# A two-layer graph network on one core: some gathers row by row from SyncE, and the turn of finished sums moved inside a unit

## The chip, the core and the metric

The kernel runs on one core of a Trainium2 chip. The metric is the device time of one execution in microseconds. Three timed runs of the kernel before gave 4084.81, 4095.0 and 4096.76 us; their median is 4095.0. The core's engines are TensorE (PE, with its weight loads as PEld), VectorE (DVE), ScalarE (ACT), GpSimd (POOL) and SyncE (SP). SyncE computes nothing here: its queue issues most of the direct transfers. ScalarE issues the stores, GpSimd the gathers.

## The reference

Two message-passing layers, each followed by a residual addition and a layer norm over the 160 features of each of N = 6250 nodes. There are E = 200000 edges, ordered by target node. A layer does this (layer 1 with 10 inputs per edge and 192 weights, layer 2 with 64 inputs and 224 weights):

```python
w   = silu(edge_inputs @ W1) @ W2              # per edge, 192 or 224 weights
g   = (x @ lin1 * node_scale)[src]             # a row of 160 per edge, gathered
mid = products of pieces of w, g and the 4 edge attributes
agg = segment_sum(mid, dst, num_segments=N) / 4
out = self_part(x) + agg @ lin2                # layer 2: then silu and a sigmoid gate
x   = layernorm(x + out)
```

Targets are drawn as 6250 u^2 of a uniform u, so low nodes have many edges, and finished nodes come faster and faster towards the end of the edge list.

## The kernel before

**Tiles and units.** The edges stand in 1563 tiles of 128; four tiles are a unit (391 units), two tiles a pair, eight tiles a chunk of edge inputs (`EC`), 48 tiles a chunk of sources and attributes (`CH`). The nodes stand in 49 blocks of 128 (the last has 106). `windows(i, ...)` (L587 to L856) runs layer i. Its loop over u (L824) is a software pipeline written out by hand; each step does, in this order:

- `gather(p)` (L697) for the two pairs of unit u+4: one indirect transfer per tile on GpSimd fetches 128 rows of 160 floats from the table in DRAM into a `g` tile (eight buffers, a pair each). The indices come from `src`, which `scalars(c)` (L602) loads with the attributes `ea` when a tile first asks for its chunk.
- `weights` (L679) for unit u+2: the second matmul of the edge network into `pw` (three PSUM buffers).
- `hidden(u+3)` (L646): the first matmul into the two `pair` buffers, and ScalarE's silu. `inputs(c)` (L625) loads the chunk after the one in use into one of three `e` buffers, through SyncE.
- for both pairs of unit u+2, `places` (L726: VectorE makes `sel`, a tile that puts each edge's attributes where its target is, in a window of 32 nodes) and `products` (L708: VectorE multiplies `g` and `pw` into `mid`, four instructions in layer 1 and six in layer 2).
- for the four tiles of unit u, `aggregate(t)` (L744): four matmuls that sum `mid` by target into `pg`. Tiles form groups of 3 to 12 that share a window; at a group's last tile ScalarE copies `pg` to `r` (L759, and to `rest` in layer 2, L765).
- `turn(g)` (L768) for the groups that ended in the unit before: two transposes on TensorE into the right half of a `pair` buffer, then a window's start loaded into a VectorE register (L778) and two additions by VectorE into the running sums `sm` and `sr` (L781, L783).
- `proceed` (L816): one step of the next block of nodes whose edges are all summed. In layer 1 the steps are `summed` (L501: seven matmuls from `sm` and `sr` into `pn`, then the residual and the norm), `turn` (L520: transposes) and `mix` (L523: the linear map of layer 2, its store to the second table by ScalarE's queue, and the store of x). In layer 2 the one step `summed` (L558) ends with the store of the output.

`prepare` (L796), called in the middle of a unit's tiles, works ahead for coming blocks: `fetch` of x, `self_part` (transposes) and `self_mix`; in layer 1 it also computes the self part of the later 25 blocks (`own_nodes`, L464) and stores it to `xown`. At most two blocks stand prepared. All of these go through one PSUM buffer, `pn`.

**What sets the order.** TensorE's instructions keep the program's order (L135 to L146); the other engines' order is the scheduler's, close to the program's. After the last unit there is one more step of the loop (`units + 1`), then the remaining turns, and then the remaining blocks, one after the other (L851 to L856). Layer 2 can gather only when the last block's rows are in the second table. Direct transfers from SyncE and ScalarE share eight counters in rotation, and each waits for the one eight places before it.

Of the kernel before, what the change touches and what calls it, by code (L numbers as in the profile page):

```python
# [28 lines left out]
BG = 4  # L29
ZERO = 8  # L30
ROWS = P * NB + P
EPS = 1e-5
# [54 lines left out]
def kernel(ctx: ExitStack, tc: tile.TileContext, a, out):  # L87
# [376 lines left out]
    def own_nodes(b, work):  # L464

        n = rows_of(b)
        rows = slice(b * P, b * P + n)
        (fetch, self_part, self_mix), _ = second_nodes(b, work, False, "ne")

        def store():  # L470
            nc.scalar.dma_start(xown[rows, :], self_mix()[:n])
            owned.add(b)

        return [fetch, self_part, store]

    def second_nodes(b, work, clear, name="nx"):
# [4 lines left out]
        st = {}  # L481

        def fetch():
            x = st["x"] = work.tile([P, D], F32, name=name, bufs=4 if name == "nx" else 1)
            if b in owned:
                nc.sync.dma_start(x[:n], xown[rows, :])
            else:
                nc.sync.dma_start(x[:n], a["x_main"][:, b, :] if b < NB - 1 else a["x_tail"])
# [12 lines left out]
        def summed():  # L501
            p = psum.tile([P, 512], F32, name="pn", bufs=1)
            q = p[:n, :2 * D].rearrange("p (w d) -> p w d", w=2)
            for c in range(4):
                l = sm[:96, c, rows]
                if c < 2:
                    matmul(q[:, :, 0:S + V], l, rm0[:, c], start=(c == 0), stop=False)
                else:
                    v = S + (c - 1) * V
                    matmul(q[:, :, 0:S], l, rm0[:, c, :, 0:S], start=False, stop=False)  # L510
                    matmul(q[:, :, v:v + V], l, rm0[:, c, :, S:], start=False, stop=False)
            matmul(q[:, :, S + V:D], sr[:64, rows], rr0, start=False, stop=True)
            y = st["x"][:n]
            for k in range(2):
                nc.vector.scalar_tensor_tensor(y, q[:, k, :], gets[:n, b, k:k + 1], y,
                                               op0=OP.mult, op1=OP.add)
            mv = work.tile([P, 8], F32, name="mv")
            normed(y, mv)

        def turn():  # L520
            st["xt"] = turned(st["x"][:n], work, "pn", 1)

        def mix():  # L523
            xt = st["xt"]
            p = psum.tile([P, 512], F32, name="pn", bufs=1)
            matmul(p[:n, 0:P], xt[:, 0, :n], who[0][:, :P], start=True, stop=True)
# [11 lines left out]
    def last_nodes(b, work, clear):  # L538
# [19 lines left out]
        def summed():  # L558
# [12 lines left out]

            gate = work.tile([P, V], F32, name="gate")
            nc.scalar.activation(gate[:n], o[:, S:96], AF.Tanh, scale=half[:n, b])
            nc.vector.tensor_scalar(gate[:n], gate[:n], 1.0, half[:n, b], op0=OP.add, op1=OP.mult)
            nc.vector.tensor_tensor(
# [3 lines left out]
            nc.vector.tensor_tensor(x, y[:n], x, OP.add)  # L579
            mv = work.tile([P, 8], F32, name="mv")  # L580
            normed(x, mv)
# [4 lines left out]

    def windows(i, loads, work, inputs_of):  # L587
        nw = (192, 224)[i]
# [36 lines left out]
        def inputs(c):  # L625
# [3 lines left out]
            k, of_e = ((10, a["e10"]), (64, a["e64"]))[i]  # L629
            e = inputs_of[c % 3]  # L630

# [47 lines left out]
        def weights(ps):  # L679
# [5 lines left out]
            for p, j in [(p, j) for p in ps for j in range(2)] if i == 0 else \  # L685
                    [(p, j) for j in range(2) for p in ps]:
                t = 2 * p + j
                if t < NT:
# [6 lines left out]
                    matmul(made["w", p][:n, j, :nw], l, r, start=True, stop=True)  # L695

        def gather(p):  # L697
            g = work.tile([P, 2, D], F32, name="g", bufs=8)
            for j in range(2):
# [96 lines left out]
        def prepare():  # L796

            if early:
                early.pop(0)()
            elif not coming and left and len(prepared) < 2:  # L800
                b = left.pop(0)
# [21 lines left out]

        for u in range(-4, units + 1):  # L824
            before = turned_to
# [31 lines left out]

# [112 lines left out]
    with tc.If(ok > 0) as cmp:  # L970
        with tc.tile_pool(name="loads", bufs=2) as loads, \
                tc.tile_pool(name="edges", bufs=2) as work:

            inputs_of = [loads.tile([P, EC * P // 2], F32, name=f"e{k}", bufs=1) for k in range(3)]
            for e in inputs_of:
                nc.vector.memset(e, 0.0)
            for i in range(2):
                windows(i, loads, work, inputs_of)
    with cmp.Else():
# [56 lines left out]
```

## Time and profile before

| what | us |
|---|---|
| median of three runs | 4095.0 |
| the profiled execution's own time | 4098.1 |
| its span, first to last instruction | 4096.3 |
| first gather of layer 1 begins | 65.8 |
| last gather of layer 1 ends | 2054.8 |
| first gather of layer 2 begins | 2089.4 |
| last gather of layer 2 ends | 4057.9 |
| last store issued (out, L582) | 4091.6 |

| stretch | PE busy | DVE busy | ACT busy | POOL busy | granted clock |
|---|---|---|---|---|---|
| 500 to 600 | 88.7 | 67.8 | 22.6 | 75.9 | 0.90 |
| 1900 to 2000 | 92.8 | 76.7 | 37.5 | 76.2 | 0.95 |
| 2300 to 2400 | 81.9 | 75.8 | 13.5 | 75.9 | 0.85 |
| 3900 to 4000 | 84.9 | 88.9 | 49.1 | 75.9 | 0.96 |

The second table gives busy microseconds in stretches of 100 us. A busy TensorE is not TensorE at its peak, since the ends of its pipelined matmuls are modelled. In the views of the trace a line reads: engine, source line, operation, tile written <- tiles read, and behind it a count, a duration in nanoseconds or microseconds, or the idle time before it in brackets with what ended it. A `q` behind an engine's name means its sequencer. GpSimd's busy time is the time in which it makes the descriptors of a gather; the transfer itself runs on the DMA engines.

### The profile page before, as it was taken

Reading aid. Unit: us, or ns where it says so; the run is one execution under the profiler, and the core shown is the slowest. Engines: PE = TensorE matmul, PEld = TensorE weight load, DVE = VectorE, ACT = ScalarE, POOL = GpSimd, SP = SyncE. Lnnn points to the kernel's source line nnn. Section 1 sums busy time; section 2 is a strip of 40 time slices with the busy share of each in tenths; the row PEclk is TensorE's granted clock in tenths of the full one; section 3 lists DMA queues with packets and bytes.
Section 4 is the critical chain, followed back from the end, with each engine's and each line's share of the span. In section 5 each row is a group of like instructions: output and inputs, shape, how many; then the busy total and the mean of one; then the engine's idle time right before and its main releaser. Section 6 shows DMA issues by size and latency. Waiting matters only on the chain. (4 is left out here: it accounts for less than half of the span.)

```text
span 4096.3 us, 108196 instructions
## 1 busy us (share of the span) xinstructions
PE 3522.1 (86%) x37363; PEld 2419.1 (59%) x37363; DVE 3095.1 (76%) x13202; ACT 1176.1 (29%) x4013; POOL 3026.7 (74%) x3232
## 2 busy tenths in 40 slices
PE   7788988889899999999978888888788888888887
PEld 5565666666666666666655555555555555555555
DVE  6676666667777777777757777777778888888887
ACT  2122221222222333333311111122223333444454
POOL 4777777777777777777757777777777777777774
PEclk8899898889899999999978888889989999998998
DMA  4233322222222232333323333333333333333332
GB/s 128 78 84 87 81 75 77 78 76 79 77 79 79 79 82 79 82 84 80 87 71 94 96 95 97 98 96 96 100 97 97 103 100 96 106 100 98 101 103 59
DMA packets 298517, 364.05 MB, mean 89 GB/s; under 512 B 86323, under 2 KB 246204, under 8 KB 297964
## 3 DMA queue, kind: packets, MB, share of 16 engines
q0 software_dynamic: 151056, 257.36, 23.8%
q1 hardware_dynamic: 121740, 85.59, 7.4%
q10 hardware_dynamic: 25168, 14.11, 1.1%
q8 instruction: 300, 4.92, 0.5%
q14 instruction: 253, 2.07, 0.2%
HBM read 338.73 MB, written 18.03 MB: 87 GB/s over the span
## 5 line engine op out<-in xcount | busy, mean ns | idle before, releaser
L703 POOL DMA_INDIRECT g<-table,src x3126 | 3004.9, 961 | 1026.8 <-issue 736.9
L721 DVE TENSOR_TENSOR mid<-g,pw 128x128 f32<-128x128 f32 (+2 forms) x7820 | 1852.8, 299 | 653.0 <-DMA g<-table,src 416.1
L138 PE MATMUL pw<-fc,h 100*128 100x192 f32 (+1 forms) x6252 | 1225.5, 383 | 193.4 <-DVE mid L721 186.4
L138 PE MATMUL pg<-mid,sel 128*32 128x160 f32 (+1 forms) x25008 | 1155.1, 305 | 0.0
L138 PEld LDWEIGHTS pw<-fc,h 100*128 100x128 f32 (+1 forms) x6252 | 895.9, 203 | 369.9 <-issue 315.0
L138 PEld LDWEIGHTS pg<-mid,sel 128*32 128x32 f32 x25008 | 755.3, 116 | 387.7 <-issue 320.7
L734 DVE SCALAR_TENSOR_TENSOR sel<-iota,off,ea 128x128 f32<-128x128 f32 x3126 | 940.5, 341 | 39.4 <-PE pg L138 35.0
L138 PE MATMUL pair<-e,fc 64*100 64x256 f32 (+1 forms) x2348 | 606.2, 454 | 120.2 <-DVE sr L783 113.4
L665 ACT ACTIVATE h<-pair 100x256 f32<-100x256 f32 x782 | 260.7, 381 | 954.6 <-PE pair L138 941.0
L138 PEld LDWEIGHTS pair<-e,fc 64*100 64x100 f32 (+1 forms) x2348 | 239.5, 183 | 351.2 <-issue 193.1
L676 ACT ACTIVATE h<-pair 128x256 f32<-128x256 f32 x392 | 150.5, 384 | 960.5 <-PE pair L138 795.6
L143 PE MATMUL pair<-ident,r 128*96 128x128 f32 (+1 forms) x852 | 225.7, 291 | 27.6 <-ACT h L665 21.7
L138 PE MATMUL pn<-rm,sm 96*128 96x128 f32 (+4 forms) x980 | 192.1, 356 | 51.2 <-DVE sm L781 49.6
L759 ACT ACTIVATE r<-pg 128x96 f32<-128x96 f32 (+1 forms) x568 | 149.5, 263 | 297.8 <-PE pg L138 228.5
L781 DVE TENSOR_TENSOR sm<-pair,sm 96x128 f32 (+1 forms) x568 | 161.9, 285 | 92.1 <-PE pair L143 19.1
L143 PEld LDWEIGHTS pair<-ident,r 128*96 128x96 f32 (+1 forms) x852 | 107.8, 127 | 206.0 <-issue 105.3
L765 ACT ACTIVATE rest<-pg 32x32 f32<-32x32 f32 x1136 | 209.5, 184 | 12.5
L138 PEld LDWEIGHTS pn<-rm,sm 96*128 96x128 f32 (+3 forms) x980 | 176.3, 235 | 59.9 <-DVE sm L781 53.3
L138 PE MATMUL pn<-rr,sr 64*128 64x128 f32 (+2 forms) x196 | 66.1, 426 | 93.4 <-DVE sr L783 89.0
L458 ACT ACT_TABLE_LOAD x97 | 124.5, 1283 | 7.1 <-DVE mv L457 5.4
L138 PEld LDWEIGHTS pair<-fold,rest 128*128 128x128 f32 x568 | 104.0, 226 | 1.1 <-ACT rest L765 1.1
L783 DVE TENSOR_TENSOR sr<-pair,sr 64x32 f32 (+1 forms) x568 | 99.7, 176 | 0.8 <-DVE sm L781 0.6
(137 smaller groups left out, 1313.0 us busy)
## 6 DMA issues: line engine op xcount, KB each, us to landing
g<-table,src POOLq DMA_INDIRECT x3126
e<-in_e SPq DMA_DIRECT2D x781, 64.0 KB
e<-in_e SPq DMA_DIRECT2D x390, 20.0 KB
ea<-in_ea_main SPq DMA_DIRECT2D x63, 96.0 KB
xg<-in_x_main SPq DMA_DIRECT2D x12, 320.0 KB
table<-rg SPq DMA_DIRECT2D x12, 320.0 KB
xmid<-nx ACTq DMA_DIRECT2D x48, 80.0 KB
table<-nr ACTq DMA_DIRECT2D x48, 80.0 KB
```

The source lines that it names most:

```text
L138: r = nc.tensor.matmul(*args, **kw)
L143: r = nc.tensor.transpose(*args)
L458: nc.scalar.activation(mv[:n, 1:2], mv[:n, 1:2], AF.Sqrt, bias=eps[:n])
L665: nc.scalar.activation(h[:100, 2 * P * j:2 * P * j + m], pair[j][:100, :m], AF.Silu)
L676: nc.scalar.activation(h[:kk, c0:c1], p[:kk, c0:c1], AF.Silu, scale=0.125)
L703: nc.gpsimd.indirect_dma_start(out=g[:n, j, :], out_offset=None, in_=table[i][:, :], in_offset=bass.IndirectOffsetOnAxis(ap=of(t)[0], axis=0))
L721: nc.vector.tensor_tensor(parts(mid[:n, :m], V * place, V * step, k), parts(g[:n, :m], c, V, k), parts(q[:n, :m], w, w_step, k), OP.mult)
L734: made["last"] = nc.vector.scalar_tensor_tensor(s[:n, j], iota[:n, None, :].to_broadcast([n, 4, W]), w, e[:, :, None].to_broadcast([n, 4, ...
L759: nc.scalar.activation(r[:, :w], pg[:, :w], AF.Copy)
L765: nc.scalar.activation(rest[g % 3][k, k], pg[k, P:P + V], AF.Copy)
L781: nc.vector.tensor_tensor(sm[:h, :, at], pt[:h, :P].rearrange("p (c w) -> p c w", c=4), sm[:h, :, at], OP.add)
L783: made["last"] = nc.vector.tensor_tensor(sr[:k, at], pt[:k, P:P + W], sr[:k, at], OP.add)
```

## The change

Four things change, in one edit.

1. **Rows through SyncE.** Units 80, 160, 240 and 320 of each layer aren't gathered by GpSimd. The rows of such a unit come one by one: `rows_of_unit` spreads 64 groups over the units since the one before it; a group loads eight indices from SBUF into SyncE's registers (`row_src`, filled at the start) and issues eight transfers of one row of 640 bytes into `gs`, a tile for a unit. These keep the program's order on SyncE.
2. **Buffers and loads.** The edge inputs have two `e` buffers instead of three. Sources and attributes of the next 48 tiles are asked for when half of the chunk is gathered. `own_nodes` uses the four `no` buffers instead of one `ne`. Up to three blocks stand prepared, with the one being computed, and four for the last.
3. **The turn.** The groups that ended in the unit before are turned between the two pairs of products, in front of the unit's own sums. `proceed` stays behind the sums and is left out in the last unit; the extra step of the loop is gone.
4. **The last blocks.** The last block works in a `pw` buffer instead of `pn`, and the remaining blocks' steps are taken in turns. In the last block of layer 2 a square root on one column stands behind the gate's tanh, ahead of the norm that needs it.

```diff
+ROW_UNITS = range(80, (NT + 3) // 4 - 1, 80)
...
-        (fetch, self_part, self_mix), _ = second_nodes(b, work, False, "ne")
+        (fetch, self_part, self_mix), _ = second_nodes(b, work, False, "no")
...
+        bank = ("pn", 1) if b < NB - 1 else ("pw", 3)
+
         def fetch():
-            x = st["x"] = work.tile([P, D], F32, name=name, bufs=4 if name == "nx" else 1)
+            x = st["x"] = work.tile([P, D if name == "nx" else 192], F32, name=name, bufs=4)[:, :D]
...
         def summed():
-            p = psum.tile([P, 512], F32, name="pn", bufs=1)
+            p = psum.tile([P, 512], F32, name=bank[0], bufs=bank[1])
...
         def turn():
-            st["xt"] = turned(st["x"][:n], work, "pn", 1)
+            st["xt"] = turned(st["x"][:n], work, *bank)
...
+            if b == NB - 1:
+
+                nc.scalar.activation(mv[:n, 8:9], gates[:n, 0, 0:1], AF.Sqrt, bias=eps[:n], scale=0.0)
...
-            e = inputs_of[c % 3]
+            e = inputs_of[c % 2]
...
+        def rows_of_unit(u):
+
+            k = next((k for k, x in enumerate(ROW_UNITS) if x - 4 >= u), None)
+            begin = 0 if not k else ROW_UNITS[k - 1] - 1
+            if k is None or u < begin:
+                return
+            x = ROW_UNITS[k]
+            if u == begin:
+                made["rows", x] = work.tile([P, 4, D], F32, name="gs", bufs=1)
+            g, steps, m = made["rows", x], x - 4 - begin, P // 2
+            for q in range((u - begin) * m // steps, min((u - begin + 1) * m // steps, m)):
+                loads_, v = nc.values_load_multi_w_load_instructions(
+                    row_src[q:q + 1, k].rearrange("q h t -> q (h t)"), engines=[ET.SP], min_val=0,
+                    max_val=N - 1,
+                    skip_runtime_bounds_check_because="an edge's source is a node")
+                for r in loads_:
+                    in_order(r)
+                for h in range(2):
+                    for j in range(4):
+                        in_order(nc.sync.dma_start(g[2 * q + h:2 * q + h + 1, j, :],
+                                                   table[i][bass.ds(v[4 * h + j], 1), :]))
+
         def gather(p):
+            if p // 2 in ROW_UNITS:
+                made["g", p] = made["rows", p // 2][:, 2 * (p % 2):2 * (p % 2) + 2, :]
+                return
...
-            elif not coming and left and len(prepared) < 2:
+            elif not coming and left and len(prepared) + bool(going) < 3 + (left[0] == NB - 1):
...
-        for u in range(-4, units + 1):
+        for u in range(-4, units):
...
-            if 0 <= u + 2 < units:
-                for p in pairs_of(u + 2):
-                    places(p)
-                    products(p)
+
+            c, at = divmod(4 * (u + 4), CH)
+            if at == CH // 2 and (c + 1) * CH < NT:
+                scalars(c + 1)
+            rows_of_unit(u)
+            ps = pairs_of(u + 2) if 0 <= u + 2 < units else []
+            for p in ps[:1]:
+                places(p)
+                products(p)
+
+            ended, waiting = waiting, []
+            for g in ended:
+                turn(g)
+                turned_to = g + 1
+            for p in ps[1:]:
+                places(p)
+                products(p)
             if u >= 0:
-                ended, waiting = waiting, []
                 for t in range(4 * u, min(4 * u + 4, NT)):
...
-                for g in ended:
-                    turn(g)
-                    turned_to = g + 1
-                proceed(turned_to if u + 3 > units else before)
+                if u < units - 1:
+                    proceed(turned_to if u + 3 > units else before)
...
-        while proceed(NG):
-            pass
+
+        chains = [going] + [steps for _, steps in prepared]
+        while any(chains):
+            for steps in chains:
+                if steps:
+                    steps.pop(0)()
...
-            inputs_of = [loads.tile([P, EC * P // 2], F32, name=f"e{k}", bufs=1) for k in range(3)]
+            inputs_of = [loads.tile([P, EC * P // 2], F32, name=f"e{k}", bufs=1) for k in range(2)]
...
+            row_src = loads.tile([P // 2, len(ROW_UNITS), 2, 4], I32, name="row_src", bufs=1)
+            for k, u in enumerate(ROW_UNITS):
+                nc.sync.dma_start(row_src[:, k], a["src_main"][:, 4 * u:4 * u + 4, 0].rearrange(
+                    "(q h) t -> q h t", h=2))
```

More of the change, by code (lines that the diff above doesn't have):

```diff
@@ L516, in summed @@
                                                op0=OP.mult, op1=OP.add)
-            mv = work.tile([P, 8], F32, name="mv")
+            mv = work.tile([P, 9], F32, name="mv")
             normed(y, mv)
         def turn():
-            st["xt"] = turned(st["x"][:n], work, "pn", 1)
+            st["xt"] = turned(st["x"][:n], work, *bank)
         def mix():
             xt = st["xt"]
-            p = psum.tile([P, 512], F32, name="pn", bufs=1)
+            p = psum.tile([P, 512], F32, name=bank[0], bufs=bank[1])
             matmul(p[:n, 0:P], xt[:, 0, :n], who[0][:, :P], start=True, stop=True)
@@ L570, in summed @@
             nc.scalar.activation(y[:n, 0:S], o[:, 0:S], AF.Silu, scale=f)
-            gate = work.tile([P, V], F32, name="gate")
-            nc.scalar.activation(gate[:n], o[:, S:96], AF.Tanh, scale=half[:n, b])
-            nc.vector.tensor_scalar(gate[:n], gate[:n], 1.0, half[:n, b], op0=OP.add, op1=OP.mult)
+            gates = work.tile([P, 2, V], F32, name="gate")
+            nc.scalar.activation(gates[:n, 0], o[:, S:96], AF.Tanh, scale=half[:n, b])
+            mv = work.tile([P, 9], F32, name="mv")
+            if b == NB - 1:
+                nc.scalar.activation(mv[:n, 8:9], gates[:n, 0, 0:1], AF.Sqrt, bias=eps[:n], scale=0.0)
+            gate = gates[:, 1]
+            nc.vector.tensor_scalar(gate[:n], gates[:n, 0], 1.0, half[:n, b], op0=OP.add,
+                                    op1=OP.mult)
             nc.vector.tensor_tensor(
@@ L579, in summed @@
             nc.vector.tensor_tensor(x, y[:n], x, OP.add)
-            mv = work.tile([P, 8], F32, name="mv")
             normed(x, mv)
@@ L584, in last_nodes, with windows @@
         return [fetch, self_part, self_mix], [summed]
-    def windows(i, loads, work, inputs_of):
+    def windows(i, loads, work, inputs_of, row_src):
         nw = (192, 224)[i]
@@ L695, in weights, with in_order @@
                     matmul(made["w", p][:n, j, :nw], l, r, start=True, stop=True)
+        def in_order(r):
+            tc.keep_in_program_order(r)
+        def rows_of_unit(u):
[18 more added lines that the diff above has]
+                                                   table[i][bass.ds(v[4 * h + j], 1), :]))
         def gather(p):
+            if p // 2 in ROW_UNITS:
+                made["g", p] = made["rows", p // 2][:, 2 * (p % 2):2 * (p % 2) + 2, :]
+                return
             g = work.tile([P, 2, D], F32, name="g", bufs=8)
@@ L972 @@
                 tc.tile_pool(name="edges", bufs=2) as work:
-            inputs_of = [loads.tile([P, EC * P // 2], F32, name=f"e{k}", bufs=1) for k in range(3)]
+            inputs_of = [loads.tile([P, EC * P // 2], F32, name=f"e{k}", bufs=1) for k in range(2)]
             for e in inputs_of:
                 nc.vector.memset(e, 0.0)
+            row_src = loads.tile([P // 2, len(ROW_UNITS), 2, 4], I32, name="row_src", bufs=1)
+            for k, u in enumerate(ROW_UNITS):
+                nc.sync.dma_start(row_src[:, k], a["src_main"][:, 4 * u:4 * u + 4, 0].rearrange(
+                    "(q h) t -> q h t", h=2))
             for i in range(2):
-                windows(i, loads, work, inputs_of)
+                windows(i, loads, work, inputs_of, row_src)
     with cmp.Else():
```

## The prediction

> **What bounds the kernel now.** I read the share of busy time first, then GpSimd's costliest group, GpSimd's waits, its instructions in order of time at the edges of the two layers, and last what TensorE and VectorE wait for late in a layer.
>
> ```profile
> PE 3522.1 (86%) x37363; PEld 2419.1 (59%) x37363; DVE 3095.1 (76%) x13202; ACT 1176.1 (29%) x4013; POOL 3026.7 (74%) x3232
> ...
> L703 POOL DMA_INDIRECT g<-table,src x3126 | 3004.9, 961 | 1026.8 <-issue 736.9
> ```
>
> TensorE has the largest share, but it isn't the bound. Of GpSimd's idle time most is "issue", which is no wait. The waits (total, times, longest) and the timeline (start, length, idle before) settle it:
>
> ```profile
> POOL g L703 <- issue: 736.9, 2417, 0.3
> POOL g L703 <- DVE mid L721: 110.3, 361, 0.5
> ...
> 65.77 1.04 POOL L703 DMA_INDIRECT g<-table,src  x1 [39.56 <-DVE rr L397]
> ...
> 2053.86 0.91 POOL L703 DMA_INDIRECT g<-table,src  x1 [0.30 <-DVE nx L515]
> 2089.39 0.96 POOL L703 DMA_INDIRECT g<-table,src  x1 [34.62 <-DMA nx<-xmid]
> ...
> 4056.89 1.00 POOL L703 DMA_INDIRECT g<-table,src  x1 [0.30 <-DVE mid L721]
> ```
>
> No gap inside a layer is over 0.5 us: 0.30 us is the pitch from one gather to the next, whatever it is put down to. GpSimd issues 1563 gathers a layer end to end and waits for nobody. So the profiled execution's own 4098.1 us is a sum: 1.8 outside the span, 65.8 to the first gather, 1989.0 of gathers (1.273 each), 34.6 without one between the layers, 1968.5 of gathers (1.260 each), and 4096.3 - 4057.9 = 38.4 after the last.
>
> How far behind are the others? In the first layer VectorE ends the last products at 2062.4, 7.6 us after the last gather was issued. In the second:
>
> ```profile
> 4074.24 0.90 DVE L721 TENSOR_TENSOR mid<-g,pw 64x64 f32<-64x64 f32 x6
> ```
>
> That ends at 4075.1, 17.2 us after GpSimd's end. Setting each pair's last product beside the end of its gather shows 3 to 5 us until 3600 (landing and products: the chain has 2.56 for a landing), then 7, 12, 13, 12 and 15: late in layer 2 TensorE and VectorE together no longer keep GpSimd's pace. GpSimd doesn't feel it, as eight `g` buffers cover 16 x 1.26 = 20 us. From 3400 to 4056 they wait for this:
>
> ```profile
> PE pn L138 <- DVE sr L783: 69.4, 26, 4.6
> PE pair L138 <- DVE sr L783: 21.1, 20, 1.7
> ...
> DVE mid L721 <- DMA g<-table,src: 15.9, 24, 1.7
> ```
>
> TensorE stands 90 us for VectorE's sums (`sr`, the end of a turn), since a block's own sums and the next hidden layer stand right behind the turn.
>
> **The change, part by part.**
>
> *Gathers gone.* Units 80, 160, 240 and 320 of each layer (16 tiles) lose their indirect gathers: 16 x 1.273 + 16 x 1.260 = **40.5 us** off the engine that paces both layers, if the others follow. VectorE's waits for gathers in layer 2 are 16 us in the last 656, and in layer 1 18 us from 1400 to 2050, so there is little to catch up with after the fourth unit of each layer. I give back 2 us; with no faster chain it would be up to 5 of each layer's 20.
>
> *Rows on SyncE.* This takes their place: 4096 one-row transfers, 4096 register operations for their addresses and 512 loads of eight indices; the whole of before has 1502 transfers on SyncE. They stand in 307 of a layer's 391 units (76, then 77 three times), 64 groups of eight rows per 77 units, so 0.83 group a unit. Prices nearby (min/median/max in ns):
>
> ```profile
> L488 SPq DMA_DIRECT2D ne<-in_x_tail x1: 247/247/247, 494.4 to 494.4; - x1
> ...
> L634 SPq DMA_DIRECT2D e<-in_e x390: 282/284/1258, 65.9 to 2022.1; - x195
> ...
> L642 SPq DMA_DIRECT2D e<-in_e x784: 282/551/1587, 2022.9 to 4036.4; - x196
> ...
> L424 SPq DMA_DIRECT2D rm<-in_lin_wv x12: 310/420/527, 34.5 to 43.9; - x12
> ...
> L781 DVEq FUSED_REGOPS  x568: 69/69/75, 98.5 to 4084.3; - x190
> ...
> L778 DVEq TENSOR_LOAD <-base x568: 297/304/601, 97.8 to 4083.7; - x190
> ```
>
> One row at a register's address isn't among them. Its ends are 0.247 (106 rows of the same 640 bytes) and 0.551 (64 rows of 1 KB); I take 0.284, the form with the fewest pieces (20). A group is then 8 x (0.284 + 0.069 + two gaps of 0.05) + 0.304 + 0.12 for the first register operation after a load (190 instead of 69) + 0.05 = 4.10 us, 3.41 a unit. SyncE's own work is 2 x 0.60 + 0.13 = 1.33 a unit in layer 2 (two edge transfers, and blocks and scalars spread over the units) and 0.47 in layer 1. Together 4.74 of 5.04 us a unit in layer 2, and 3.88 of 5.09 in layer 1: it fits, **at 94%**, so I cost it at nothing. What hides it is SyncE's spare time. Queued behind the rows are the edge inputs that TensorE waits for in program order; these now have two buffers instead of three, so they can be issued once TensorE has read the chunk before last, with three units (15 us) to land. With 0.247 the unit is 4.5 us, with 0.551 it is 6.5, far over. Each row also waits for the transfer eight places before it (eight counters shared with ScalarE): eight rows take 3.6 us, a landing 2.5, so that wait is covered; a stalled SyncE would hold up ScalarE's stores too.
>
> The Trainium skill ("DMA: Bandwidth & Descriptors", Latency and other measured facts) speaks against a queue full of index loads: it gives a register load from SBUF a floor of about 600 ns. The 568 loads on VectorE's sequencer had a median of 304, SyncE's single one (the flag, L969) 564. By the page's figure a group costs 0.3 more, an estimate of 0.25 a unit, and SyncE would stand at 99% in layer 2.
>
> *Sums turned in front of a unit's own sums.* The transposes and VectorE's two additions move from the unit's end to between its two pairs of products; the block's sums stay last. So VectorE can add while TensorE runs the unit's 32 matmuls (1.3 us), and most of the 90 us of waits goes. In a stretch that GpSimd paces that is worth nothing. Where the chain lags it is what counts: I take the lag at the end of layer 2 from 17.2 to about 8, what layer 1 ends with: **-9.5 us** in the tail. Bounds: 0 (another wait takes its place: VectorE is busy 176 of 200 us from 3800) and -14.
>
> *Between the layers.* Today the last two turns and block 48's sums stand behind the turn of block 47:
>
> ```profile
> 2073.14 0.59 PE L143 MATMUL pn<-ident,nx 128*128 128x128 f32 x2 [2.92 <-DVE nx L460]
> 2073.53 1.18 PE L143 MATMUL pair<-ident,r 128*96 128x128 f32 x4
> ...
> 2076.47 3.11 PE L138 MATMUL pn<-rm,sm 96*106 96x192 f32 x12 [0.48 <-ACT nr L529]
> ```
>
> After the change the turns come right behind the last tile (whose copy ends at 2070.7), and block 48 has PSUM buffers of its own (`pw`), so its sums start when 47's transposes end, at 2073.7 instead of 2076.5: **-2.8 us** of the 34.6. The rest of 48's path (sums, norm, transposes, store, landing) is as long as before. In the last tail 48's sums already start straight after the last turn, and ScalarE's table load for the square root (4089.11, 1.28 long) ends before VectorE's statistics (4090.61): the load moved forward hides nothing there. I take 0; at worst 48 stands behind 47's sums, +3.
>
> *Cost nothing:* four index loads at the start (4 x 0.6, on SyncE, while GpSimd already gathers), chunks of scalars asked for half a chunk ahead, one more block prepared, the `no` buffers: all on queues that GpSimd doesn't wait for. They would cost if they delayed the first products by over 20 us.
>
> **Sum.** 4098.1 - 40.5 + 2 - 9.5 - 2.8 = 4047.3 in the profiled execution's terms. That execution is 3.1 above the median of the three runs (4084.8 to 4096.8), so 4044.
>
> **The rivals.**
>
> *The chain gets no faster* (0.18). GpSimd's 40.5 us are gained where it paces, but late in layer 2 TensorE and VectorE set the end: the last unit's 5 us and the tail's 9.5 aren't gained. 4098.1 - 40.5 + 5 + 2 - 2.8 - 3.1 = 4059. For it: VectorE's 88% from 3800, of which few waits name `sr`. Against: TensorE's 90 us.
>
> *SyncE becomes the bound; slower* (0.14). Its place is the SP queue in layer 2's 307 units with rows; the price is its surplus over 5.04 a unit; it decides from a row transfer of 0.33 us, and as about three units of slack (15 us) spread over 77 forgive 0.2 a unit, it hurts from 0.36. With 0.420, L424's form, a group is 5.19, a unit 4.31 + 1.33 = 5.64, and 307 x 0.60 = 184 us more: 4044 + 184 = 4228. With 0.551 the same sum gives a unit of 6.51, 307 x 1.47 = 451 us, and in layer 1 5.18 + 0.47 = 5.65, 307 x 0.56 = 172: 4667, the far end. For it: back to back, 32-row forms took 0.42. Against: all forms of few pieces were at 0.25 to 0.28, and a register operation stands between two rows.
>
> *It doesn't do what it says* (0.06). Rows come late now and then, at 94 to 100% of SyncE: edge inputs land after TensorE asks for them, and the 20 us of buffers are used up and given back four times a layer. Eight times 5 us is all that the gathers gave: about 4085.
>
> **How the numbers follow.** Forecast 0.62, rivals 0.18, 0.14 and 0.06. Low end: tail -14, 2 us not given back, layers' gap -5, and a run as fast as the fastest of before (10 below the median): 4044 - 4.5 - 2 - 2.2 - 10 = 4025. High end 4085: it takes in the chain that gets no faster and most of the late rows, and leaves out SyncE as the bound. A measurement of this kernel can tell 0.3% from no change, 12 us: faster is below 4083, with 0.82; same 0.04; slower 0.14.
>
> **What would show it.** 3094 gathers still 1.25 to 1.27 us apart, none waiting inside a layer; a step of four missing gathers at eight places. On SyncE a row transfer under 0.33 us (0.25 to 0.28 would fit best) and no unit over 5 us; TensorE without waits for edge inputs or `gs`. TensorE's wait for `sr` well under half of 90 us from the same stretch, and the last products some 8 us after the last gather. Layers' gap about 32 us. Wrong if VectorE waits for `gs`, if GpSimd waits for products late in layer 2, or if a row transfer takes over 0.36 us.

## The result, and the profile after

The change made the kernel slower: 4292.7 us, median of four runs (4269.4 to 4311.2), beside 4093.9 for the kernel before on the same chip. The ratio is 1.0492, 95% interval 1.0454 to 1.0529. The forecast was 4044. The profiled execution took 4288.5, span 4286.7. In the changed kernel lines of before move: the gather is L739, products L757, `sel` L770, hidden's silu L673 (layer 1) and L684 (layer 2), a turn's sums L817 and L819, a row's load of indices L719 and its transfer L727.

Busy shares, and GpSimd's group in the costliest groups of the page (busy time, mean ns | idle time and its largest share):

```profile
PE 3482.7 (81%) x37363; PEld 2391.6 (56%) x37363; DVE 3099.0 (72%) x13201; ACT 1180.6 (28%) x4014; POOL 2997.6 (70%) x3200
...
L739 POOL DMA_INDIRECT g<-table,src x3094 | 2975.8, 962 | 1247.8 <-issue 717.4
```

The 32 gathers are gone and one costs what it did (962 ns, 961 before), but GpSimd's idle time rose from 1026.8 to 1247.8 us. Every engine has a smaller share: something makes them wait for each other. GpSimd's waits (total, times, longest):

```profile
POOL g L739 <- DVE mid L757: 326.0, 414, 8.7
```

Before, the longest of these was 0.5 us, little over the usual gap of 0.3. Now GpSimd stands up to 8.7 us for VectorE's products: a `g` buffer isn't free, so the products are 20 us behind. Summed over the gaps longer than 0.5 us, and without the 0.3 us that every gap has, GpSimd waited 173 us in layer 1 and 46 in layer 2. The sum of before, term by term:

| us | before | after |
|---|---|---|
| first to last gather, layer 1 | 1989.0 | 2137.5 |
| no gather, between the layers | 34.6 | 45.3 |
| first to last gather, layer 2 | 1968.5 | 2001.9 |
| after the last gather | 38.4 | 36.2 |

What does VectorE wait for? TensorE, and TensorE in turn for this (its waits, the changed kernel):

```profile
PE pair L144 <- ACT h L673: 231.1, 253, 4.3
PE pair L144 <- ACT h L684: 148.8, 187, 3.1
PE pn L144 <- DMA nx<-xmid: 126.5, 25, 10.6
...
PE pn L144 <- DMA nx<-in_x_main: 65.7, 12, 9.3
PE pair L139 <- DMA e<-in_e: 51.5, 23, 5.9
...
PE pn L139 <- DVE sr L819: 6.9, 9, 1.0
```

The last line is what the prediction wanted: waits for a turn's additions (`sr`) are all but gone. The others are two new families. The first: a turn's transposes (`pair`, L144) wait for ScalarE's `h`: 253 times in layer 1's 284 turns, 187 times in layer 2's 284. The second: TensorE waits for transfers that SyncE issues, a block's x (`nx`) and the edge inputs (`e`).

The timeline shows the first (start, length, idle before it in brackets):

```profile
1503.89 0.68 PE L139 MATMUL pair<-e,fc 64*100 64x256 f32 x4
...
1504.66 0.66 ACT L673 ACTIVATE h<-pair 100x256 f32<-100x256 f32 x2 [1.77 <-PE pair L139]
...
1505.10 0.46 PE L144 MATMUL pair<-ident,r 128*96 128x128 f32 x2 [0.53 <-ACT h L673]
...
1505.65 0.29 DVE L817 TENSOR_TENSOR sm<-pair,sm 96x128 f32 x1 [0.63 <-ACT h L673]
```

The hidden layer writes the left half of a `pair` buffer, ScalarE reads it into `h`, and the turn writes the right half of the same buffer. In both kernels the program makes the turn wait for that reading. Before, the unit's own 32 matmuls stood between hidden and turn, and `h` was done in time. Now the turn stands right behind hidden: TensorE stops 0.53 us, and VectorE 0.63, since its additions stand between its two pairs of products.

Layer 2 of the same trace shows that it is the buffer and not the place alone. There hidden writes only `pair[u % 2]`, and the turn of group g uses `pair[g % 2]`. Counted in the order of TensorE's instructions, 192 of the 284 turns fall in the buffer that hidden has just written, and 187 of them waited for `h`. The other 92 stand in the same place but in the other buffer, and none of them waited for it.

The second family starts on SyncE. From the timeline of the changed kernel, first SyncE's own (a line's length includes the gaps within its group), then a line of ScalarE's queue and one of TensorE:

```profile
573.26 21.72 SPq L727 DMA_DIRECT2D gs<-table  x16
...
605.58 3.51 SPq L727 DMA_DIRECT2D gs<-table  x8
609.14 0.37 SPq L491 DMA_DIRECT2D nx<-in_x_main  x1
```

```profile
588.47 0.34 ACTq L534 DMA_DIRECT2D xmid<-nx  x1
```

```profile
611.13 0.69 PE L144 MATMUL pn<-ident,nx 128*128 128x128 f32 x2 [6.40 <-DMA nx<-in_x_main]
```

Sixteen rows took 21.7 us, where 7.3 to 7.7 stand elsewhere in the timeline without such a wait: one of them, issued at 590.1, had waited 14.4 us for the store of `xmid`, which ScalarE issued only at 588.5. What stands behind the rows comes later: the next block's x is asked for at 609.1, and TensorE, which should transpose it, stands 6.4 us.

### The profile page after: what moved, and what is told of

Same layout as the page of the kernel before. It is cut to its first block, busy times and chain, and to the rows that moved or that the text cites. A ratio compares the mean times of both kernels' runs of the same rounds, so it can differ in the third digit from the quotient of the medians.

```text
span 4286.7 us, 121016 instructions
## 1 busy us (share of the span) xinstructions
PE 3482.7 (81%) x37363; PEld 2391.6 (56%) x37363; DVE 3099.0 (72%) x13201; ACT 1180.6 (28%) x4014; POOL 2997.6 (70%) x3200
## 5 line engine op out<-in xcount | busy, mean ns | idle before, releaser
L739 POOL DMA_INDIRECT g<-table,src x3094 | 2975.8, 962 | 1247.8 <-issue 717.4
L757 DVE TENSOR_TENSOR mid<-g,pw 128x128 f32<-128x128 f32 (+2 forms) x7740 | 1841.2, 298 | 449.2 <-PE pw L139 254.1
L139 PE MATMUL pw<-fc,h 100*128 100x192 f32 (+1 forms) x6252 | 1201.0, 389 | 92.3 <-DVE mid L757 72.6
L139 PE MATMUL pg<-mid,sel 128*32 128x160 f32 (+1 forms) x25008 | 1166.9, 306 | 0.0
L770 DVE SCALAR_TENSOR_TENSOR sel<-iota,off,ea 128x128 f32<-128x128 f32 x3126 | 939.9, 341 | 282.8 <-PE pg L139 251.9
L139 PE MATMUL pair<-e,fc 64*100 64x256 f32 (+1 forms) x2348 | 583.7, 448 | 57.0 <-DMA e<-in_e 51.5
L144 PE MATMUL pair<-ident,r 128*96 128x128 f32 (+1 forms) x852 | 228.5, 293 | 381.0 <-ACT h L673 231.1
L673 ACT ACTIVATE h<-pair 100x256 f32<-100x256 f32 x782 | 258.3, 380 | 969.3 <-PE pair L139 948.0
L144 PEld LDWEIGHTS pair<-ident,r 128*96 128x96 f32 (+1 forms) x852 | 109.1, 128 | 617.8 <-ACT h L673 344.5
L684 ACT ACTIVATE h<-pair 128x256 f32<-128x256 f32 x392 | 150.0, 383 | 816.4 <-PE pair L139 702.7
L817 DVE TENSOR_TENSOR sm<-pair,sm 96x128 f32 (+1 forms) x568 | 162.8, 287 | 289.0 <-ACT h L673 111.5
L144 PE MATMUL pn<-ident,nx 128*128 128x128 f32 (+1 forms) x242 | 69.6, 382 | 214.7 <-DMA nx<-xmid 126.5
L144 PEld LDWEIGHTS pn<-ident,nx 128*128 128x128 f32 (+1 forms) x242 | 22.5, 143 | 258.5 <-DMA nx<-xmid 137.6
L139 PE MATMUL pn<-rm,sm 96*128 96x128 f32 (+3 forms) x968 | 151.6, 305 | 0.0
L139 PEld LDWEIGHTS pn<-rm,sm 96*128 96x128 f32 (+2 forms) x968 | 138.5, 194 | 12.6 <-issue 9.8
L441 ACT ACTIVATE xt<-pn 128x128 f32<-128x128 f32 (+1 forms) x146 | 40.3, 276 | 350.1 <-PE pn L144 341.8
```

Source lines behind the costliest of these rows:

```text
L139: r = nc.tensor.matmul(*args, **kw)
L144: r = nc.tensor.transpose(*args)
L441: nc.scalar.activation(xt[:, 0, :n], p[:, 0:n], AF.Copy)
L673: nc.scalar.activation(h[:100, 2 * P * j:2 * P * j + m], pair[j][:100, :m], AF.Silu)
L684: nc.scalar.activation(h[:kk, c0:c1], p[:kk, c0:c1], AF.Silu, scale=0.125)
L739: nc.gpsimd.indirect_dma_start(out=g[:n, j, :], out_offset=None, in_=table[i][:, :], in_offset=bass.IndirectOffsetOnAxis(ap=of(t)[0], axis=0))
```

## The experiments

**Two theories and the rival.** T: the turn behind hidden costs the time. R: the rows cost it, by what they hold back on SyncE. S: SyncE's plain occupation, the rival on record. The change was first taken apart: each half alone, neither, and the turn in a third place. Ratios are to the kernel before on the same chip (before: 4094 here, 4099 with the next four), since chips differ.

*turn_back* (rows kept):

```diff
-            ended, waiting = waiting, []
-            for g in ended:
-                turn(g)
-                turned_to = g + 1
...
                         waiting.append(group_of[t][0])
+                for g in ended:
+                    turn(g)
+                    turned_to = g + 1
```

> The changed kernel with one thing undone: a group's turn stands behind the unit's own sums again, as before the change; rows on SyncE, two edge buffers, scalars ahead and the last blocks stay. Theory T (the turn): moved forward, the transposes stand right behind the hidden layer's matmuls and wait on TensorE for ScalarE's h, which sits in the same PSUM tile (231 + 345 + 149 us of waits on h on TensorE in the changed kernel's trace, and 112 us on VectorE), so TensorE falls behind GpSimd, which then waits 222 us for buffers. By T undoing the move gives the forecast back: 4045 to 4065, and GpSimd waits for products under 20 us. Theory R (the rows): rows wait on SyncE for ScalarE's stores through the shared counters (137 + 115 + 61 + 33 us), block fetches and edge inputs come late, TensorE stands 192 + 52 us for them; by R this kernel stays at 4250 to 4300. Theory S (the rival on record, SyncE's own throughput): 4230 to 4290 as well, with SyncE's queue never idle.

*no_rows* (turn in front kept): `ROW_UNITS = ()`.

> The changed kernel without rows on SyncE: all 3126 gathers on GpSimd again, everything else of the change kept, the turn in front of the unit's sums too. T: TensorE sets the pace in layer 1, so the time stays near the changed kernel's, 4240 to 4300, with GpSimd still waiting over 150 us for products. R and S: 4080 to 4095, as before the change less a few us at the end of the layers. If both T and R hold in part and add up, 4150 to 4220.

*neither*: both edits.

> The changed kernel with both undone: no rows, the turn behind the unit's sums. What is left of the change: two edge buffers instead of three, scalars asked for ahead, one more block prepared, own buffers for the last block's sums, the square root's load forward. T, R and S all expect 4083 to 4097 (before: 4094). Above 4110 it would be the small edits, the third edge buffer first, that cost.

*turn_mid* (rows kept):

```diff
                 for t in range(4 * u, min(4 * u + 4, NT)):
+                    if t == 4 * u + 2 or (t == min(4 * u + 4, NT) - 1 and u == units - 1):
+                        for g in ended:
+                            turn(g)
+                            turned_to = g + 1
+                        ended = []
```

> The changed kernel with the turn in the middle of the unit's own sums: after two of the unit's four tiles (16 matmuls, 0.65 us behind the hidden layer), so that h has time to be done, and VectorE's additions stand behind both pairs of products. Rows kept. T: waits for h on TensorE fall to under a third, and the time goes to 4040 to 4065, as with the turn at the unit's end or a little under it. R and S: 4250 to 4300, no better than the change.

| kernel | time | ratio, 95% | GpSimd's waits, layers 1 / 2 | TensorE waits for h | for sr | for nx, no | for e |
|---|---|---|---|---|---|---|---|
| before | 4094 | 1 | 0 / 0 | 31 | 203 | 32 (`ne`) | 6 |
| changed | 4293 | 1.0492 (1.0454 to 1.0529) | 173 / 46 | 397 | 11 | 214 | 51 |
| turn_back | 4128 | 1.0076 (1.0051 to 1.0101) | 40 / 26 | 46 | 119 | 271 | 73 |
| no_rows | 4186 | 1.0243 (1.0210 to 1.0277) | 70 / 4 | 388 | 35 | 0 | 16 |
| neither | 4089 | 0.9987 (0.9977 to 0.9998) | 0 / 0 | 40 | 225 | 0 | 28 |
| turn_mid | 4112 | 1.0047 (1.0027 to 1.0067) | 42 / 4 | 105 | 97 | 247 | 67 |

(The last five columns are from one profile each. GpSimd's waits are counted as above. The 345 us in turn_back's text are weight loads that stand for the same `h` as the matmuls; they aren't added here.) T and R both hold, in part each. Over *neither* the turn alone costs 97 us and the rows alone 39; together they cost 204, 68 more than the sum. *neither* came as all expected, so the small edits cost nothing. No theory by itself was right: T's number for *turn_back* (4045 to 4065) was missed by 63 us and its number for *no_rows* (4240 to 4300) by 54, R's for *no_rows* (4080 to 4095) by 91 and R's and S's for *turn_back* (4230 or more) by over 100. *no_rows* lies where both in part were said to put it. The fourth kernel shows that it is the place behind hidden: sixteen matmuls further on, the waits for `h` are a quarter and 181 us are gone, against a loss of 199. T's 4040 to 4065 was missed by 47; *mid_no_rows* below shows that this is the rows again. Two things stay open. This edit also moves VectorE's additions behind both pairs of products (in the changed kernel's layer 1 they waited 112 us for `h`), so it doesn't part TensorE's stop from VectorE's. And a turn with a PSUM buffer of its own wasn't tried.

TensorE's waits with the turn in front and no rows, and then with neither:

```profile
PE pair L144 <- ACT h L673: 233.0, 254, 3.8
...
PE pair L144 <- ACT h L684: 149.8, 188, 3.1
```

```profile
PE pair L144 <- ACT h L673: 30.5, 27, 2.6
...
PE pair L144 <- ACT h L684: 4.3, 7, 1.0
```

Here is why *neither* doesn't wait, from TensorE's timeline, with the unit's 32 matmuls between hidden and turn:

```profile
1499.76 0.68 PE L139 MATMUL pair<-e,fc 64*100 64x256 f32 x4
1500.37 1.27 PE L139 MATMUL pg<-mid,sel 128*32 128x160 f32 x32
1501.57 0.46 PE L144 MATMUL pair<-ident,r 128*96 128x128 f32 x2
```

Why more than the sum? The end of a pair's products behind the end of its gather (mean of some 30 pairs) suggests a reason. In layer 1, in pairs 520 to 549, this lag is 5 us with neither, 17 with rows alone, 19 with the turn alone, 23 with both; eight `g` buffers hold 20. A wait of TensorE under that cover costs nothing, and past it the whole of it. By this reading the turn's small waits eat the cover that the rows' long ones need, and the other way round. No run varied the cover by itself, so this account of the 68 us fits the lags but isn't shown. After the last unit by rows, to the layer's end, the lag falls to 6 or 7 with rows alone and stays at 20 with both, as with the turn alone.

**What in the rows costs?** The next four kernels, on another chip, vary the rows, with the turn in the middle:

*mid_half*: `ROW_UNITS = range(160, (NT + 3) // 4 - 1, 160)`.

> The turn in the middle of the unit's own sums, and half the rows: only units 160 and 320 of each layer by rows, so one group of eight rows in two units or so; 16 gathers fewer in all, worth 20 us. Theory Q (the rows hold back what stands behind them on SyncE: a block's fetch and the edge inputs land late, and TensorE stands 313 us for them with all rows, 28 us without): with half the rows TensorE waits under 110 us for these, GpSimd waits for nobody inside a layer, and the time is 4062 to 4080. Theory C (GpSimd's gathers are simply as fast as the chain behind them can go, so that fewer gathers gain nothing): 4085 to 4095. A linear price of the rows, from 4089 without to 4111 with all: 4100.

*mid_act*: in `fetch`, three lines like

```diff
-            nc.sync.dma_start(x[:n], xmid[rows, :])
+            nc.scalar.dma_start(x[:n], xmid[rows, :])
```

> The turn in the middle, all rows, and the blocks' fetches (nx and no, some 150 transfers) asked for on ScalarE's queue instead of SyncE's, so that they no longer stand behind rows. Q: the 247 us in which TensorE stands for nx and no with the turn in the middle go to under 60, and the time to 4050 to 4080. Theory B2 (the rows' own waits on the shared counters for ScalarE's stores, and the edge inputs behind them, are what costs): 4095 to 4115, with TensorE's waits moved from nx to e. If ScalarE itself now stands for buffers of nx, its silu comes late and the time is over 4115.

*mid_e3*: `inputs_of[c % 3]` again, `g` with 7 buffers, `no` with 3, and `< 2 + (left[0] == NB - 1)`: the third edge buffer is paid for with a `g` buffer, a `no` buffer and one prepared block.

> The turn in the middle, all rows, and three edge buffers as before the change; their room comes from one gather buffer (7 instead of 8), one buffer of no (3 instead of 4) and one block prepared less (2, as before the change). Theory L (with two edge buffers SyncE can't run ahead: each request waits until TensorE has read the chunk before last, 217 + 181 + 73 us of SyncE's waits, and the rows of two units and the fetch come after that): with a third buffer SyncE is a chunk, 10 us, ahead, TensorE's 313 us of waits for nx, no and e fall to under 100, and the time to 4055 to 4080. If lookahead isn't it, 4105 to 4125, the smaller depth a little on the bad side.

*mid_no_rows*: the turn in the middle and `ROW_UNITS = ()`.

> The turn in the middle without rows, as a base for the others. GpSimd paces both layers with all gathers, so 4080 to 4095 by every theory; what it can show is whether the turn in the middle costs anything by itself (over 4100: it does) and how far the products lag behind the gathers late in a layer: 17 us late in layer 2 before the change.

| kernel | time | ratio, 95% | layer 1 / layer 2, gathers | GpSimd's waits | TensorE waits for nx, no | for e |
|---|---|---|---|---|---|---|
| mid_no_rows | 4099 | 0.9997 (0.9987 to 1.0006) | 1994.8 / 1968.2 | 0 / 0 | 0 | 21 |
| mid_half | 4077 | 0.9950 (0.9934 to 0.9967) | 1980.8 / 1961.2 | 0 / 0 | 0 | 17 |
| mid_act | 4125 | 1.0058 (1.0040 to 1.0075) | 2005.1 / 1982.5 | 31 / 27 | 0 | 236 |
| mid_e3 | 4108 | 1.0021 (1.0010 to 1.0031) | 2000.1 / 1971.0 | 26 / 11 | 237 | 61 |

*mid_half* is Q's number: half the rows give their 20 us and no wait for nx or no is left. So a row isn't dear in itself. Whether their number or their density counts it can't tell, as it halves both; the last kernel below bears on that. *mid_act* refuted Q's simple form: the waits for nx went, as Q said, and came back as waits for e, as B2 said (1.0058 of 4094 is 4118, 3 us over its range). The third case, ScalarE standing for buffers of nx, was put at over 4115 too; but TensorE's waits for `h` are 119 us instead of 105, too little to be it. *mid_e3* (theory L) left TensorE's waits at 298 us, though the ratio is 0.26% under turn_mid's on another chip. That third buffer alone isn't the cure; as the kernel gives up lookahead elsewhere, it doesn't refute lookahead as such. By *mid_no_rows* the turn in the middle costs nothing that can be seen by itself (its 4099 is over the range of 4080 to 4095 as this chip's before is 5 us longer).

So SyncE itself is late. In layer 2 that is plain; SyncE's longest waits from 2200 to 3600, first with neither, then with the turn in the middle and all rows:

```profile
SPq L650 <- PE pair L139: 529.4, 176, 11.4
SPq L619 <- DMA g<-table,src: 393.8, 71, 18.2
```

```profile
SPq L727 <- DMA out<-nx: 24.9, 9, 9.4
SPq L650 <- PE pair L139: 14.4, 30, 3.4
```

Without rows SyncE waits for TensorE to free an edge buffer (529 of 1400 us): it is early. With them that falls to 14. Instructions and the gaps under 0.15 us between them fill 1347 of the 1400 us, 96%, where without rows it was 28%. In layer 1 they fill about 76% (200 to 1600), and the rest is largely waits of rows and edge inputs for stores that ScalarE issues at a unit's end (turn in the middle, all rows):

```profile
SPq L727 <- DMA xmid<-nx: 114.0, 20, 13.3
SPq L727 <- DMA table<-nr: 70.2, 21, 10.0
```

**Less in front of the fetch.** Two edits test this: an empty step between a block's `fetch` and its first use, so that it is asked for one unit earlier (theory F, layer 1), and sixteen indices for one load (theory O, occupation).

```diff
-        return [fetch, self_part, self_mix], [summed]
+        return [fetch, lambda: None, self_part, self_mix], [summed]
...
-            g, steps, m = made["rows", x], x - 4 - begin, P // 2
+            g, steps, m = made["rows", x], x - 4 - begin, P // 4
...
-                for h in range(2):
+                for h in range(4):
```

The fetch edit is made in layer 1's steps too, `row_src` gets four rows of four indices a partition, and the early square root uses an existing column (`mv` is [P, 8] again).

> The turn in the middle, all rows, and a block's fetch asked for one unit earlier (an empty step between fetch and first use), still on SyncE. Theory F (in layer 1 SyncE has time to spare, 28 to 60 us of 200 idle in each stretch with rows, but each group of rows waits for a store that ScalarE issues only at the unit's end, and the fetch stands right behind the rows with one unit to land): 5 us more are enough in layer 1, TensorE's waits for nx and no (86.8 and 32.5 us) go to under 30, and layer 1's gathers take 1970 to 1985 us instead of 2010. Theory O (occupied: in layer 2 SyncE is busy 196 of 200 us from 2200 to 3600, so what it asks for is late however early it stands in the queue): layer 2 stays at 1966 +- 8. Both: 4075 to 4090. If neither, 4105 to 4115.

> The turn in the middle, all rows, with sixteen indices for one register load instead of eight: 256 loads on SyncE instead of 512 (0.8 us each in the trace), the rows themselves unchanged. O: SyncE's occupation in layer 2 falls from 98% to about 92%, TensorE's waits for nx<-xmid and e in layer 2 go to under half, and layer 2's gathers from 1966 to 1955 or less; layer 1 gains little (2000 to 2010). Time 4085 to 4105. If a load of sixteen takes twice as long as one of eight, nothing moves: 4105 to 4115.

> Both of the former: the fetch one unit earlier and sixteen indices for a load. If F holds for layer 1 and O for layer 2, this has the gathers at pace in both layers: 1970 to 1980 and 1950 to 1958, and a time of 4050 to 4070, faster than the kernel before. If only one holds, 4075 to 4095.

> The turn behind the unit's own sums as before the change, and half the rows (units 160 and 320 of each layer). With no rows this order took 4089, the turn in the middle 4099 to 4094; half the rows gave 20 us with the turn in the middle. So 4065 to 4075 if the two add; over 4085 if the waits for late transfers come back with this order.

With these four kernels, and with their four repeats, TensorE was granted 0.75 to 0.78, and the kernel before took 5925 to 6038 us. GpSimd waits 910 to 1000 us a layer for products then, so it isn't what paces the layers, and a gather saved can't shorten them. Ratios: mid_fetch 1.0051, mid_16 1.0205, mid_f16 1.0044 (one chip); repeats 1.0009 for mid_fetch_b, 0.9984 for mid_f16_b, 1.0028 for mid_f16_c. The turn behind the sums lost too: back_half 1.0139 (1.0114 to 1.0164) and back_half_b 1.0109, with 445 and 418 us of waits for sr. None of this tells what half the rows with that order would do at 0.90. One comparison does hold, on one chip: from mid_16 to mid_f16, the fetch one unit earlier, waits for nx and no fall from 198 to 64 us, those for e rise from 9 to 53, and the ratio falls by 1.6%.

> The kernel of mid_fetch again (turn in the middle, all rows, a block's fetch one unit earlier), on a chip that grants TensorE about 0.90 like the first ten runs. The call before ran where the kernel before takes 5931 us at a granted clock of 0.765, TensorE sets every unit's time and GpSimd waits 950 us a layer, so it can't weigh rows against gathers. F (layer 1: fetch and rows wait for ScalarE's stores, SyncE has time to spare) expects layer 1's gathers at 1970 to 1985 us instead of 2010 and TensorE's waits for nx and no under 60 in all; O (layer 2: SyncE occupied) expects layer 2 unchanged at 1966 +- 8 with waits for e in place of those for nx. Both: 0.995 to 1.000 of before. Neither: 1.0047 as before.

> The kernel of mid_f16 again: fetch one unit earlier and sixteen indices a load. The trace of mid_16 has 1.276 us for a load of sixteen against two of 0.805, so a unit in layer 2 needs 0.14 us less of SyncE, 3% of its 4.9. O: layer 2's gathers 1955 to 1965, a little under mid_fetch_b; F as there. 0.990 to 0.998 of before.

> The kernel of back_half again: turn behind the unit's sums, half the rows. On the chip with a clock of 0.765 this order lost 1.4%, with TensorE waiting 445 us for VectorE's sr. At a clock of 0.90, GpSimd paces and 20 us of gathers are gone: 0.992 to 0.996 of before, as mid_half's 0.995; over 0.999 if late transfers come back with this order.

> The kernel of mid_f16 once more (turn in the middle, all rows, fetch one unit earlier, sixteen indices a load), since the last call's chip again granted TensorE 0.765 (6038 us for the kernel before). At a clock of 0.90: F expects layer 1's gathers at 1970 to 1985 us instead of 2010, O layer 2's at 1955 to 1965, and TensorE's waits for nx, no and e under 110 in all instead of 313: 0.990 to 0.998 of before. If the rows cost through something else, 1.003 to 1.006 like turn_mid. At 0.765 again: 0.997 to 1.005, which tells nothing of it.

The last repeat of mid_f16 had a clock of 0.92 (the kernel before on this chip: 0.90, 4103 us):

> The kernel of mid_f16 a last time (turn in the middle, all rows, fetch one unit earlier, sixteen indices a load). What the low clock did show: with sixteen indices, asking for the fetch one unit earlier took TensorE's waits for nx and no from 198 to 63 us and 1.6% off the time (mid_16 1.0205, mid_f16 1.0044, same call). At a clock of 0.90, F expects layer 1's gathers at 1970 to 1985 us (turn_mid: 2010), O layer 2's at 1955 to 1965 (1966), and 0.990 to 0.998 of before; 1.003 to 1.006 if the rows cost through something else. At 0.765: 0.998 to 1.005, of which nothing follows.

4077 us, 0.9926 (0.9897 to 0.9955): faster than the five kernels above with all 4096 rows at a clock near 0.90 (1.0021 to 1.0492). Layer 2 took 1954.8 us, inside O's 1955 to 1965 but for the last digit, with 2 us of GpSimd's waits; SyncE was filled 94% from 2200 to 3600. Layer 1 took 1992.1, not F's 1970 to 1985, with 18 us of waits instead of 42. TensorE's waits for nx and no fell from 247 to 93, those for e rose from 67 to 98: 192 in all, where under 110 was expected (in mid_f16_c's text). The two edits weren't separated at this clock.

Last, the same rows spread thinner (`ROW_UNITS = range(94, (NT + 3) // 4 - 1, 94)`; before on this chip: 4096):

> The kernel of mid_f16 with the same four units by rows in each layer, but every 94th instead of every 80th, so that the same 4096 rows are spread over 363 units a layer instead of 307 (91 instead of 77 units for one unit's rows): 15% less of SyncE's time for rows in each unit. Q and O (what the rows hold back on SyncE is what costs): layer 1's gathers, 1992 us with 18 us of GpSimd's waits in mid_f16_d, come to 1972 to 1982, layer 2's, 1955, to 1950 to 1956; TensorE's waits for nx, no and e from 191 to under 130 us; 0.986 to 0.991 of the kernel before. If the number of rows costs and not their density, 0.992 to 0.995. On a chip that grants 0.765, 0.995 to 1.003.

4061 us, 0.9913 (0.9897 to 0.9930), the lowest time of all. SyncE is filled 85% from 2200 to 3600. GpSimd's waits beyond the pitch are gone (1972.6 and 1953.5 us of gathers), as the longest in its waits for products shows, and TensorE waits 50 us for nx, no and e in all:

```profile
POOL g L739 <- DVE mid L757: 95.5, 313, 0.3
```

The layers' times came as expected if density counts. The ratio lies just above the 0.986 to 0.991 that this theory gave, and its interval overlaps mid_f16_d's, so the times alone don't decide; the waits, 50 us instead of 192 with the same number of rows, speak for density.

## Why the prediction was wrong, point by point

**Gathers gone, -40.5: right where nothing waits.** spread94's gathers take 1972.6 and 1953.5 us, 37 less than mid_no_rows' and 26 less than *neither*'s: the pitch of a gather differs between runs by up to 0.006 us (1.270 to 1.276 in layer 1), 9 us a layer, so the term is known no better than that.

**"Rows on SyncE ... I cost it at nothing": failed.** The sizes were close: a row 0.228 (0.284 was taken), its register operation 0.037 (0.069) with a move of 0.029 that I hadn't listed, the load 0.805 (0.304).

```profile
L727 SPq DMA_DIRECT2D gs<-table x4096: 224/228/307, 86.0 to 3890.0; - x196
```

```profile
L719 SPq TENSOR_LOAD <-row_src x512: 685/805/1241, 85.1 to 3886.0; - x171
```

A group is 4.35 (median pitch of two groups with nothing between) instead of 4.10; with the 1.33 of the prediction a unit in layer 2 is 4.95 of 5.04, 98%. The floor of about 600 ns for a `tensor_load`, which I weighed from the Trainium skill ("DMA: Bandwidth & Descriptors", Latency and other measured facts) and didn't take, was nearer than VectorE's 304. SyncE's loads agree with it, 685 at the least in this trace; VectorE's 297 before lie under it. But the step that failed is the inference. "It fits, at 94%, so I cost it at nothing" treats a queue as free until it is full. What stands behind the rows is late already when the queue has no time left to catch up: TensorE's 25 waits for nx<-xmid in the changed kernel are 5 us in the mean and 10.6 at most. In layer 1, where SyncE had a quarter to spare, the sentence on the eight counters failed: "that wait is covered", with "a stalled SyncE would hold up ScalarE's stores". It is the other way round: rows wait for stores that ScalarE issues only at a unit's end, 61 to 137 us in the changed kernel for each of xmid, table and xown. How much of the time in layer 1 this is worth beside SyncE's occupation no run parts. The price was 39 us over *neither* instead of -38: 77 us mis-sized.

**The rival "SyncE becomes the bound" was nearer in its place than in its price.** Its 4228 came from a row of 0.420, which isn't so, and at 0.228 its own threshold said that it can't decide. Its place, SyncE in layer 2, is shown. "Rows late now and then", about 4085, named the edge inputs but not the blocks' fetches, which were four times as much, and was given 0.06.

**The turn in front, -9.5: failed, and the largest term.** I looked for what waited for the turn and not for what the turn waits for. The waits for sr went (203 us in the whole run before, of which the prediction's 90 are a part; 11 after), and 366 us of new ones for h came. My lower bound of the term was 0, "another wait takes its place"; it was +97 alone. The lag at the end of layer 2, which I took from 17.2 to 8, was 17.9 with the turn in front, changed kernel and *no_rows* alike, and 9.4 in *neither*, where the turn hadn't moved. So the turn in front doesn't shorten it. With the turn in the middle it is 15.4 without rows and 9.7 with them, so one profile of each can't say what does.

**The two together: a term that was missing.** Over the forecast of 4044 the rows are 77 us mis-sized, the turn 107, and 68 more come from having both; 77 + 107 + 68 = 252, beside the 249 that were missed.

**Between the layers, -2.8: right, and hidden.** From the last products of layer 1 to the first gather of layer 2 it is 27.0 us before, and 23.3 to 25.5 in every kernel with the last block's own buffer at a clock near 0.90. The 45.3 of the changed kernel has 21.7 us of lag in front of it.

**"Cost nothing": right for the time, wrong for the tail.** Buffers, scalars ahead, one more block prepared and the last blocks side by side give 0.9987 together, and *neither*'s tail is 29.5 us instead of 38.4. Which of them does it wasn't tried; over the kernels with the change's ends at a clock near 0.90 tails lie between 28.0 and 36.9, so one profile each can't tell.

**What the text said would prove it wrong** was GpSimd waiting for products late in layer 2. It did wait in layer 2, 46 us, but layer 1 lost three quarters of the time: I had taken layer 1's lag of 4 to 8 us for safety.

## What to carry to other kernels

When an instruction is moved earlier, list what it waits for, by buffers and not by data: a tile shared by two halves couples them, and the work that it is moved past may be what hid that wait. A queue that is 94% full isn't free: ask what stands behind the new transfers, when it is needed and what else the new ones wait for; spreading the same rows over more units took TensorE's waits behind them from 192 to 50 us. And two delays that draw on one cover, here 20 us of gather buffers, can cost more together than the sum of each alone: 204 us instead of 136.

## What the runs showed of the hardware that I had not expected

- A load of indices into SyncE's registers took 0.805 us for eight (median) and 1.289 for sixteen, while VectorE's loads of one value took 0.304: 0.16 us saved for eight indices.
- A row transfer at a register's address is cheap on SyncE: 0.228 us, no more than transfers at fixed addresses (0.247 to 0.284).
- In three of the seven sets of runs TensorE was granted about 0.765 instead of about 0.90, and the kernel before took 5925 to 6038 us instead of 4094. GpSimd's gathers and VectorE's products were as long as ever (0.964 and 0.344 us in mid_fetch, 0.965 and 0.352 in turn_mid); a kernel paced by GpSimd in one set isn't in another, and what a version gains changes with it (mid_f16 is at 0.9926 with a clock of 0.92, at 0.9984 to 1.0044 with 0.765). The clock alone is a sixth less and the time 45% more: TensorE's idle time rose too, from 642 us in turn_mid to 1492 in mid_fetch, over 800 of them gaps that the profile puts down to no wait. Why, the runs don't show.
